# A row LSTM over images on one core: every 64-row product of the steady part made as two products of 64 output columns

## The chip, the cores and the metric

The kernel runs on one core of a Trainium2 chip. What is measured is the device time of one execution in microseconds. Engines are named as in the profile: PE is TensorE (PEld its weight loads), DVE is VectorE, ACT is ScalarE, POOL is GpSimd, SP is SyncE, which issues the DMA transfers.

## What is computed

The input x has 8 images of 96 channels, 128 rows and 128 pixels, in float32. It is normalised in 32 groups of channels per image. A masked convolution along each row makes four gates for every channel, and an LSTM runs down the rows: row r needs the hidden state h of row r - 1, through another convolution of three taps. The output is x plus all h.

```python
x = x + _L0_conv_ref(_gn(x), W_is, b_is, W_ss, b_ss)

its = conv(X, W_is * mask) + b_is            # 96 -> 384 channels, 1 x 3, causal in the pixels
def step(carry, row_in):                     # once for each of 128 rows
    h, c = carry
    ss = conv(h, W_ss) + b_ss                # 96 -> 384 channels, 3 taps
    gates = ss + row_in
    g5 = gates.reshape(B, 3, 4, Oc, Wd)      # Oc = 32: three thirds, four gates
    f, i, o = sigmoid(g5[:, :, 0]), sigmoid(g5[:, :, 1]), sigmoid(g5[:, :, 2])
    g = tanh(g5[:, :, 3])
    c_new = f * c + i * g
    h_new = o * tanh(c_new)
    return (h_new, c_new), h_new
```

The rows are a chain of 128 steps, and all arithmetic is float32.

## The kernel before

**Half-steps.** The eight images are two sets of four. A half-step is one row of one set: `HalfStep(n)` for n from -2 to 255, even n for the first set, odd n for the second (the first is one row ahead). While one set's elementwise work runs, the other set's products do. The code writes the order of the instructions of PE, ACT, DVE and POOL by hand: the string `PERIOD` (line 775) lists the pieces of a half-step with marks for which half-step they belong to, and `do` (line 803) issues them in that order. Lines 1175 and 1176 do so for n from 2 on; the last half-step has its own list.

**Products.** The 384 gate channels are three tiles A, B, C of 128, each with a PSUM bank of its own per half-step (`ps`, 128 partitions by 512 values: 256 for one half of the pixels, 256 for the other). The three-tap convolutions are rewritten over pairs of pixels, so that each tile takes seven kinds of products: "1", "2", "0" and "3" from the hidden state (moving operands `vs`, `vf` and the two parts of `vd`, made on DVE and POOL, lines 639 to 650), and "P", "Q" and "E" from the input (`xs`). All go through `HalfStep.mm` (lines 482 to 500, the matmul at 492): `rows` says which partitions of the weights and of the moving operand take part.

**Lanes.** In the steady part no product uses all 128 rows of the array. `piece` (line 508) makes each of "1", "2", "0", "3" as two products of 64 rows, one of partitions 0 to 63 and one of 64 to 127, and each of "P", "Q", "E", whose operand is 64 channels, as one product of 64 rows; `xs` holds these channels twice, so that either half of the rows will do. The class `Lanes` (line 407) chooses the half, mostly by the marks `<` and `>` in `PERIOD`, so that products of both halves alternate. Where two products in a row write the same bank from different halves, `mm` lets the later one wait until the earlier has ended (lines 489 to 491): `self.writer[a]` keeps the rows of the bank's last product and its number.

**After the products.** ACT adds the bias and copies one half of a bank (`copy`, line 563), DVE adds and subtracts (`even`, `odd`, lines 567 and 571), ACT makes tanh and sigmoid (lines 575, 587), DVE and POOL the cell (lines 592 to 611), ACT its tanh, DVE h (line 624), and DVE and POOL the moving operands of the next row. SP issues all transfers.

Of the kernel before, what the change touches and what calls it, by code (L numbers as in the profile page):

```python
# [21 lines left out]
def kernel(  # L22
# [29 lines left out]
    nc = tc.nc  # L52
    B, C, H, W = x.shape
    P = 128
    NH = 2
# [193 lines left out]
    class Scale:  # L249
# [23 lines left out]
        def mm(self, o, i, rhs, start=False, stop=False):  # L273
            nc.tensor.matmul(o, gm[:, i, :], rhs, start=start, stop=stop, skip_group_check=True)  # L274
# [110 lines left out]
    HB = BH * J  # L385
    NT = NB * R
    last = NT * NH - 1
# [54 lines left out]
    def hold(made, until):  # L442
        if until.ins.engine != E.Pool:
# [6 lines left out]
                reason="GpSimd starts when VectorE is done with both SBUF reads",  # L450
            )

    residuals = []
    lanes = Lanes()
    whole = slice(0, P)

    class HalfStep:
# [24 lines left out]
        def mm(self, a, half, weights, rhs, rows=slice(0, P)):  # L482
            self.take_bank(a)
            new = a not in self.started
            self.started.add(a)

            lo, hi = self.images.get(a, (0, BH))
            cols = slice(lo * J, hi * J)
            before = self.writer.get(a)
            if before is not None and before[0] != rows and whole not in (before[0], rows):  # L490
                lanes.wait(before[1])
            made = nc.tensor.matmul(  # L492
                self.ps[a][:, bass.ts(half, HB)][:, cols],
                weights[rows, bass.ts(a, P)],
                rhs[rows, cols],
                start=new,
                stop=False,
                skip_group_check=True,
            )
            self.writer[a] = rows, lanes.issued(made)  # L500

        def own(self, a, i):
# [579 lines left out]
    n = m = 0  # L1082
# [39 lines left out]
    rows = ring[2][:, 0 : (R - 1) * BH * (W + 1)].rearrange("p (r q) -> p r q", q=W + 1)  # L1122
# [109 lines left out]
```

## Time and profile before

| what | value |
|---|---|
| three runs | 1959.95, 1960.5, 1963.89 us; median 1960.5 us |
| the profiled execution | span 1964.8 us; no other time of it is given |
| PE, PEld busy | 1907.0 us (97%), 1821.3 us (93%), 17450 instructions each |
| DVE, ACT, POOL busy | 1799.9 us (92%), 1566.5 us (80%), 1354.5 us (69%) |
| granted TensorE clock, mean | 0.996 |
| line 492 in the chain that ended last | 93% |
| DMA | 234.64 MB, mean 119 GB/s |

The page shows the busy time of each engine, the same in 40 slices of the span, and the chain of work that ended last, followed back from the end: what stands in it set the time. A group of instructions is a line with what is written and read, the count, the busy time together, the mean length of one and the idle time before. In the groups of PE, "64*128" are the rows and columns of the array, and "64x256" partitions and columns of the moving operand. The timeline gives start and length of single instructions or of runs of equal ones. Matmuls are pipelined: the recorded length of one reaches into the next, and starts tell more than lengths.

### The profile page before, as it was taken

Reading aid. Unit: us, or ns where it says so; the run is one execution under the profiler, and the core shown is the slowest. Engines: PE = TensorE matmul, PEld = TensorE weight load, DVE = VectorE, ACT = ScalarE, POOL = GpSimd, SP = SyncE. Lnnn points to the kernel's source line nnn. Section 1 sums busy time; section 2 is a strip of 40 time slices with the busy share of each in tenths; the row PEclk is TensorE's granted clock in tenths of the full one; section 3 lists DMA queues with packets and bytes.
Section 4 is the critical chain, followed back from the end, with each engine's and each line's share of the span. In section 5 each row is a group of like instructions: output and inputs, shape, how many; then the busy total and the mean of one; then the engine's idle time right before and its main releaser. Section 6 shows DMA issues by size and latency. Waiting matters only on the chain.

```text
span 1964.8 us, 46182 instructions
## 1 busy us (share of the span) xinstructions
PE 1907.0 (97%) x17450; PEld 1821.3 (93%) x17450; DVE 1799.9 (92%) x4014; ACT 1566.5 (80%) x3501; POOL 1354.5 (69%) x1645
## 2 busy tenths in 40 slices
PE   3799999999999999999999999999999999999998
PEld 0469999999999999999999999999999999999997
DVE  5788999999999999999999999999999999999998
ACT  6678888888888887887888788888888878888886
POOL 3447777777777777777777777777777777777751
PEclk9989999999999999999999999999999999999999
DMA  9994424544443454444345443434544443354411
GB/s 401 412 300 101 113 73 113 119 98 101 100 110 89 100 119 98 109 92 115 86 97 119 98 116 88 116 89 90 119 104 112 92 108 96 84 119 111 106 33 33
DMA packets 101293, 234.64 MB, mean 119 GB/s; under 512 B 5840, under 2 KB 7376, under 8 KB 95056
## 3 DMA queue, kind: packets, MB, share of 16 engines
q1 hardware_dynamic: 101072, 231.70, 45.5%
q8 instruction: 138, 2.26, 0.5%
q14 instruction: 83, 0.68, 0.1%
HBM read 181.34 MB, written 50.33 MB: 118 GB/s over the span
## 4 chain that ended last, share of the span: by engine, by line
PE 94%; DMA 3%; ACT 1%; DVE 1%; issue 0%; POOL 0%; SPq 0%; DVEq 0%; POOLq 0%; ACTq 0%
PE ps L492 93%; DMA xs<-in_x_dram 3%; DVE bst L1113 1%; PE rows L198 0%; ACT xs L239 0%; ACT xs L240 0%; ACT g L575 0%; PE dm L183 0%; PE pv L274 0%; DVE hx L624 0%; ACT ps L587 0%; SPq L1100 0%; ACT piece L239 0%; POOL xw L320 0%; PE rows L183 0%
## 5 line engine op out<-in xcount | busy, mean ns | idle before, releaser
L492 PE MATMUL ps<-vd,wl 64*128 64x256 f32 (+1 forms) x6080 | 1190.5, 376 | 2.0 <-DVE ps L571 2.0
L492 PEld LDWEIGHTS ps<-vd,wl 64*128 64x128 f32 (+1 forms) x6080 | 870.8, 186 | 21.1 <-DVE ps L571 4.6
L492 PE MATMUL ps<-vs,wm 64*128 64x256 f32 (+1 forms) x3046 | 821.3, 377 | 2.9 <-POOL vs L639 2.2
L492 PE MATMUL ps<-vf,wm 64*128 64x256 f32 (+1 forms) x3046 | 767.0, 377 | 0.1
L492 PE MATMUL ps<-xs,wx 64*128 64x128 f32 (+1 forms) x3582 | 747.2, 348 | 1.8 <-POOL xs L337 1.8
L492 PEld LDWEIGHTS ps<-xs,wx 64*128 64x128 f32 x3582 | 605.6, 188 | 7.5 <-POOL xs L337 3.3
L587 ACT ACTIVATE ps<-ps 96x512 f32<-96x512 f32 (+1 forms) x768 | 388.4, 506 | 227.6 <-PE ps L492 219.0
L492 PEld LDWEIGHTS ps<-vs,wm 64*128 64x128 f32 (+1 forms) x3046 | 529.0, 186 | 13.9 <-POOL vs L639 3.4
L575 ACT ACTIVATE g<-ps 32x256 f32<-32x256 f32 (+1 forms) x1021 | 468.8, 482 | 19.3 <-PE ps L492 0.6
L492 PEld LDWEIGHTS ps<-vf,wm 64*128 64x128 f32 (+1 forms) x3046 | 460.3, 186 | 20.2 <-DVE vf L643 1.1
L492 PE MATMUL ps<-xs,wt 64*128 64x256 f32 x1518 | 449.3, 377 | 0.0
L563 ACT ACTIVATE m<-ps,wl 128x256 f32<-128x256 f32 x766 | 363.2, 474 | 102.8 <-PE ps L492 78.4
L647 POOL TENSOR_TENSOR vd<-hx 128x512 f32<-128x512 f32 x257 | 287.8, 1120 | 179.5 <-DVE vs L639 172.0
L567 DVE TENSOR_TENSOR ps<-m,ps 128x256 f32<-128x256 f32 x768 | 324.3, 423 | 82.4 <-ACT m L563 82.3
L571 DVE TENSOR_TENSOR ps<-m,ps 128x256 f32<-128x256 f32 x768 | 327.2, 426 | 17.7
L665 DVE TENSOR_TENSOR x<-x,hx 96x512 f32<-96x512 f32 x253 | 339.6, 1342 | 0.0
L320 POOL TENSOR_SCALAR xw<-xr,rstd,nmr 128x512 f32<-128x512 f32 (+1 forms) x264 | 207.5, 787 | 127.0 <-DVE x L665 113.9
L320 POOL TENSOR_SCALAR hx<-x,rstd,nmr 32x512 f32<-32x512 f32 (+1 forms) x244 | 218.9, 897 | 77.1 <-POOL xs L341 53.5
L341 POOL TENSOR_TENSOR xs<-xw 128x512 f32<-128x512 f32 (+1 forms) x254 | 271.2, 1068 | 0.0
L492 PEld LDWEIGHTS ps<-xs,wt 64*128 64x128 f32 x1518 | 264.8, 187 | 0.9 <-issue 0.3
L599 POOL TENSOR_TENSOR g<-i,g 96x256 f32<-96x256 f32 x251 | 182.5, 727 | 119.0 <-ACT g L575 110.6
L616 ACT ACTIVATE th<-c 96x256 f32<-96x256 f32 (+1 forms) x509 | 191.4, 419 | 2.7 <-DVE c L611 2.3
(101 smaller groups left out, 1506.0 us busy)
## 6 DMA issues: line engine op xcount, KB each, us to landing
xr<-in_x_dram SPq DMA_DIRECT2D x124, 512.0 KB, 6.9
x<-in_x_dram SPq DMA_DIRECT2D x62, 768.0 KB, 7.4
out_dram<-x SPq DMA_DIRECT2D x62, 768.0 KB, 4.7
xs<-in_x_dram SPq DMA_DIRECT2D x31, 1024.0 KB, 10.7
piece<-in_x_dram SPq DMA_DIRECT2D x16, 1024.0 KB, 10.8
x<-in_x_dram SPq DMA_DIRECT2D x62, 256.0 KB, 4.8
out_dram<-x SPq DMA_DIRECT2D x2, 576.0 KB, 3.7
xs<-in_x_dram SPq DMA_DIRECT2D x2, 512.0 KB, 8.2
```

Source lines behind the costliest of these rows:

```text
L320: return engine.tensor_scalar(dst, src, scale, shift, ALU.mult, ALU.add)
L341: engine.tensor_sub(differences, strided(xw[:, 0, :], 0, [(W + 1, n), (J, 2), (1, J)]), strided(xw[:, 0, :], J + 1, [(W + 1, n), (0, 2), ( ...
L492: made = nc.tensor.matmul(self.ps[a][:, bass.ts(half, HB)][:, cols], weights[rows, bass.ts(a, P)], rhs[rows, cols], start=new, stop=False, ...
L563: nc.scalar.activation(self.m1[a], m1, AF.Identity, bias=column)
L567: nc.vector.tensor_add(self.ps[a][:, 0:HB], self.m1[a], self.ps[a][:, HB:])
L571: nc.vector.tensor_sub(hi, self.m1[a], hi)
L575: nc.scalar.activation(self.part(g, lo, hi, t), self.part(ps, lo, hi, t), AF.Tanh)
L587: nc.scalar.activation(to, gate, AF.Sigmoid)
L599: nc.gpsimd.tensor_mul(to, i, g)
L616: nc.scalar.activation(self.part(self.th, lo, hi, t), self.part(self.c, lo, hi, t), AF.Tanh)
L647: diff = nc.gpsimd.tensor_sub(self.operand("vd", 2)[:, :, lo:hi], strided(h, 1, [(BH * JP - 1, 2), (JP, hi - lo), (1, J)]), strided(h, 0, ...
L665: residuals.append(nc.vector.tensor_add(xo, xo, self.h))
```

## The change

In half-steps 3 to 253 (`n_split`: `NH` is 2 and `last` is 255) each product of 64 rows is issued as two. The first takes the first 64 of the tile's 128 weight columns and writes partitions 0 to 63 of the bank, the second takes the other 64 columns and writes partitions 64 to 127. Both read the same 64 rows of the same moving operand, and both start or add to the bank's sums as the one did. The bank's last writer is now the second of the two. Products outside these half-steps, and products of 128 rows, are issued as before.

```diff
+    def n_split(n):
+        return NH < n < last - 1
+
...
             before = self.writer.get(a)
             if before is not None and before[0] != rows and whole not in (before[0], rows):
                 lanes.wait(before[1])
-            made = nc.tensor.matmul(
-                self.ps[a][:, bass.ts(half, HB)][:, cols],
-                weights[rows, bass.ts(a, P)],
-                rhs[rows, cols],
-                start=new,
-                stop=False,
-                skip_group_check=True,
-            )
+            parts = 2 if rows != whole and n_split(self.n) else 1
+            for q in range(parts):
+                wide = P // parts
+                made = nc.tensor.matmul(
+                    self.ps[a][bass.ts(q, wide), bass.ts(half, HB)][:, cols],
+                    weights[rows, bass.ds(a * P + q * wide, wide)],
+                    rhs[rows, cols],
+                    start=new,
+                    stop=False,
+                    skip_group_check=True,
+                )
             self.writer[a] = rows, lanes.issued(made)
```

On PE, the place where half-step 28 ends its products of `vs` and half-step 29 has begun those of `xs`: `ps2_0_15` is the bank of tile C of the first set in row 15, `ps1_1_14` and `ps2_1_14` are banks of the second set in row 14, and the shape is that of what is written. Before:

```order
L492 MATMUL ps2_0_15_3055<-vs_0_15_3110,wm_66 128x256
L492 MATMUL ps1_1_14_3108<-xs11_77,wx_67 128x256
L492 MATMUL ps2_1_14_3144<-xs11_77,wx_67 128x256 [waits PE_49,Activation_49]
L492 MATMUL ps2_0_15_3055<-vs_0_15_3110,wm_66 128x256 [waits PE_49]
L492 MATMUL ps2_1_14_3144<-xs11_77,wx_67 128x128
L492 MATMUL ps0_0_15_3084<-xs01_75,wt2_65 128x256 [waits DVE_49]
```

The same six products after the change:

```order
L498 MATMUL ps2_0_15_3890<-vs_0_15_3962,wm_66 64x256 x2
L498 MATMUL ps1_1_14_3959<-xs11_77,wx_67 64x256 x2
L498 MATMUL ps2_1_14_4013<-xs11_77,wx_67 64x256 [waits PE_49,Activation_49]
L498 MATMUL ps2_1_14_4013<-xs11_77,wx_67 64x256
L498 MATMUL ps2_0_15_3890<-vs_0_15_3962,wm_66 64x256 [waits PE_49]
L498 MATMUL ps2_0_15_3890<-vs_0_15_3962,wm_66 64x256
L498 MATMUL ps2_1_14_4013<-xs11_77,wx_67 64x128 x2
L498 MATMUL ps0_0_15_3928<-xs01_75,wt2_65 64x256 [waits DVE_49]
L498 MATMUL ps0_0_15_3928<-xs01_75,wt2_65 64x256
```

The order of the products stays; each stands there twice, the two halves one behind the other, and a wait stays on the first of them. The other engines keep their instructions and their order.

## The prediction

> **What bounds the kernel now.** I read the whole page first (engine totals, the slices, the chain that ended last), then the chain in order of time, then one half-step in the timeline. The page and the chain:
>
> ```profile
> span 1964.8 us, 46182 instructions
> PE 1907.0 (97%) x17450; PEld 1821.3 (93%) x17450; DVE 1799.9 (92%) x4014; ACT 1566.5 (80%) x3501; POOL 1354.5 (69%) x1645
> PE   3799999999999999999999999999999999999998
> PEclk9989999999999999999999999999999999999999
> ...
> 161.88 7.49 PE ps L492 x66
> 169.40 1772.87 PE ps L492 x16396
> 1942.31 5.46 PE ps L492 x34
> ```
>
> From 169.4 us to 1942.3 us the chain is nothing but matmuls of line 492: no wait for another engine stands in it for 1772.87 us, and the clock is at full speed. VectorE at 92% is a close second by share, but nothing in this stretch waits for it on the path. TensorE's "busy" alone would not tell that it is at its limit, so the next view is a stretch of the timeline, first the matmuls, then the weight loads:
>
> ```profile
> 827.29 0.38 PE L492 MATMUL ps<-vd,wl 64*128 64x256 f32 x1
> 827.39 0.38 PE L492 MATMUL ps<-vs,wm 64*128 64x256 f32 x1
> 827.50 0.38 PE L492 MATMUL ps<-vf,wm 64*128 64x256 f32 x1
> 827.61 0.38 PE L492 MATMUL ps<-vs,wm 64*128 64x256 f32 x1
> 827.72 0.38 PE L492 MATMUL ps<-vf,wm 64*128 64x256 f32 x1
> 827.82 0.38 PE L492 MATMUL ps<-vd,wl 64*128 64x256 f32 x1
> 827.93 0.38 PE L492 MATMUL ps<-vs,wm 64*128 64x256 f32 x1
> 828.04 0.38 PE L492 MATMUL ps<-vd,wl 64*128 64x256 f32 x1
> ```
>
> ```profile
> 827.39 0.19 PEld L492 LDWEIGHTS ps<-vs,wm 64*128 64x128 f32 x1
> 827.50 0.19 PEld L492 LDWEIGHTS ps<-vf,wm 64*128 64x128 f32 x1
> 827.72 0.18 PEld L492 LDWEIGHTS ps<-vd,wl 64*128 64x128 f32 x1
> 827.72 0.18 PEld L492 LDWEIGHTS ps<-vs,wm 64*128 64x128 f32 x1
> 827.83 0.19 PEld L492 LDWEIGHTS ps<-vd,wl 64*128 64x128 f32 x1
> ```
>
> One product of the program is two records here: the totals have 17450 matmuls and as many loads for half as many products. I call each record a pass. The passes of two products are woven into each other: vs at 827.39 and 827.61 is one product in one half of the rows of the array (a lane), vf at 827.50 and 827.72 another in the other lane. Within a lane the starts are 0.22, 0.21 and 0.22 us apart (827.39, .61, .82, 828.04; and 827.50, .72, .93), though each pass is recorded as 0.38 us long, so the recorded length overlaps its successor. The rate is what counts: 16396 passes in 1772.87 us over two lanes are 2 x 1772.87 / 16396 = 0.216 us per pass and lane. The lanes run without gaps; that is the bound.
>
> The loads tell the other half. Each starts with a matmul's start (827.50 beside 827.50) or a hair behind it, and runs under that matmul: it fills the lane for the next pass. Where its data come late (the two at 827.72, one of which would have been due at 827.61) the matmul behind it still starts at its place, 827.82. So a load is hidden as long as it is sent while the pass before it runs.
>
> What a load costs when nothing hides it is seen in one place, the start, where products of 64 columns are shorter than their loads:
>
> ```profile
> 144.06 0.52 PEld L492 LDWEIGHTS ps<-xs,wx 64*128 64x128 f32 x8 [0.33 <-issue]
> ...
> 144.50 0.19 PEld L492 LDWEIGHTS ps<-xs,wt 64*128 64x128 f32 x1
> 144.50 0.19 PEld L492 LDWEIGHTS ps<-xs,wx 64*128 64x128 f32 x1
> 144.61 0.19 PEld L492 LDWEIGHTS ps<-xs,wt 64*128 64x128 f32 x1
> 144.62 0.19 PEld L492 LDWEIGHTS ps<-xs,wx 64*128 64x128 f32 x1
> ```
>
> Eight loads, four in each lane, take from 144.06 to 144.50, and the next follow 0.11 us later: a load of 64 rows by 128 columns holds its lane 0.11 us, of which the recorded 0.19 is the longer, overlapping form.
>
> **The change part by part.** How many products are split comes from the groups that keep shapes apart:
>
> ```profile
> L492 PE MATMUL ps<-vd,wl 64*128 64x256 f32 x6016 | 1174.5, 376 | 0.0
> L492 PE MATMUL ps<-vs,wm 64*128 64x256 f32 x3012 | 809.6, 376 | 0.1
> L492 PE MATMUL ps<-vf,wm 64*128 64x256 f32 x3012 | 755.8, 377 | 0.1
> L492 PE MATMUL ps<-xs,wx 64*128 64x256 f32 x2562 | 594.7, 379 | 1.8 <-POOL xs L337 1.8
> L492 PE MATMUL ps<-xs,wt 64*128 64x256 f32 x1518 | 449.3, 377 | 0.0
> L492 PE MATMUL ps<-xs,wx 64*128 64x128 f32 x1004 | 191.3, 271 | 0.0
> ...
> L492 PE MATMUL ps<-xs,wh 64*128 64x256 f32 x36 | 7.7, 479 | 0.1
> ```
>
> The 256-wide groups sum to 16156 passes, 8078 products, and 50 of these lie outside the steady part and stay whole (the program's order has 50 unsplit ones); the 128-wide one is 502 products, all split. So 8530 products become 17060, and 17060 passes become 34120, each with a load of its own.
>
> 1. The work in the array. A pass of a half has the same 256 moving columns, so I keep 0.216 us for it. If the two halves, which use the same rows but different columns of the array, run at the same time, this term is zero; if they take turns in their lane, every product costs its lane 0.432 us more. No row shows two products in the same rows at once. I take zero, because two products in different rows do run at once above without lengthening each other, and price the other end as a rival.
>
> 2. The loads. The halves are written one behind the other: load, matmul, load, matmul of the left half, then the same of the right. If a lane takes its instructions in this order, the second pass of the left half must wait 0.216 us for the first, and only when it has started is the right half's first load sent. That load has nothing to hide under in its own columns: these are idle and wait for it. The same happens at each change from one half to the other. So each of the 17060 halves pays one exposed load. Bounds: 0 if the load is sent early; 0.19 if it costs what is recorded for one. I take half of the measured 0.11, 0.055 us, since half the columns are loaded and this row is the nearest (if the time of a load does not depend on its columns it is 0.11). A product then holds its lane 2 x (0.216 + 0.055) = 0.542 in place of 0.432, +0.110 us. For a 128-wide one: now load-bound at 2 x 0.11 = 0.22, then 2 x (0.11 + 0.055) = 0.33, +0.11 too. Sum: 8530 x 0.110 over two lanes = 469 us.
>
> 3. Instructions to fetch and send. Per pass TensorE must be handed a load and a matmul; today such a pair every 1772.87 / 16396 = 0.108 us suffices, afterwards a pair each 0.054 us would be needed to keep pace with the array, or 0.068 with term 2. The eight pairs at 144.06 went out in 0.44 us, 0.055 each, but they were few, and came after a wait of 0.33 us. So the price per pair lies between 0.055 and 0.108 us, and the time from nothing to the doubling of the steady part. I take nothing: the nearest row is the 0.055, below the 0.068 that term 2 leaves. It is the second largest doubt.
> The Trainium skill bears on this: "TensorE: Matmul & The Clock Gate", section "Wait — 56ns, not 53.3ns?", has about 62 ns of the sequencer per MATMUL where the hardware decoder is off, as the bound once a matmul is shorter than that. By that figure 34120 matmuls take 2115 us and the whole about 2285 (an estimate by that page) in place of term 2's sum; the trace cannot show which decoder is on, only that a load and a matmul together fit into 108 ns.
>
> 4. Waits and the other engines. The waits stay on the first of the two halves and their number is the same; what is behind a waiting load in the queue is now twice as many instructions but the same products. The second half ends a bank later than the product did, so ScalarE's and VectorE's readers start later by at most one pass per product chain. Those are off the path as long as TensorE is the slower, and slower it gets: VectorE's 1799.9 us of work gains slack. Nothing charged. The cover is TensorE's own slowness; without it VectorE would be next, at 92%.
>
> 5. The start before 160 us and the last half-steps keep their whole products: nothing.
>
> Sum, in the profiled execution: 1964.8 + 469 = 2434 us; the median of the runs, 1960.5, lies 4.3 below this execution, so I forecast **2430 us**. The half-step shows it directly:
>
> ```profile
> 1000.98 0.73 POOL L599 TENSOR_TENSOR g<-i,g 96x256 f32<-96x256 f32 x1 [0.23 <-ACT g L575]
> ...
> 1008.12 0.73 POOL L599 TENSOR_TENSOR g<-i,g 96x256 f32<-96x256 f32 x1 [0.44 <-ACT g L575]
> ```
>
> GpSimd's one product per half-step recurs after 7.14 us; with 251 half-steps, 469 us more make it 9.0.
>
> **The rivals.**
> - Not slower. All four quarters of the array run at once and each right-half load is sent while the left half still works. Place: the loads of the right half start with, or before, the left half's second matmul. Then a pass stays 0.216 and the time stays 1960; only the 1004 narrow passes lose their load bound (0.11 to about half of 0.216), at most 1 us. It decides if the array takes a load for idle columns past a matmul that still waits, as it now takes the loads of one lane past the other lane's waiting matmul (both loads at 827.72 are sent before either lane's next matmul). Against it: that jump is between rows, not within them. A real gain needs the pass itself to get below 0.216: I know of no row for that, and give 1% (20 us) as its size.
> The Trainium skill, "TensorEngine Tiling (Array Packing)", section "Tiling Modes", Key Properties, says of four 64x64 tiles that they are independent and may load and multiply in parallel; by that rule this rival holds and the sum is 1960 instead of 2430. The trace agrees for tiles in different rows and shows none in the same rows.
> - Taking turns. The two halves of a product share one stream of moving data per lane and run one after the other: 8028 x 0.432 + 502 x 0.22 us over two lanes, +1789, so 3750. For it: nothing in the trace has two streams in the same rows. Against: it would make the column position useless.
> - Bound by issue. At a price p per pair the steady part takes 34120 x p: with the 171 us around it (1960.5 - 1789) 0.07 gives 2560, 0.09 gives 3240, 0.105 gives 3750.
> - A smaller loss, 0.2% to 10% (up to 2160): loads partly hidden, or semaphores that fire later because the right half ends later.
>
> **How the numbers follow.** Exposed loads: 0.38, with 0.04 to 0.07 us per load 2300 to 2560. Bound by issue: 0.20. Taking turns: 0.13. A smaller loss: 0.08. All four at once with no change: 0.15; with a gain: 0.06. Under 0.2% a difference cannot be told from none here (the three runs spread by that). Faster 0.06, same 0.15, slower 0.79. Leaving out turns (0.13) and the gain (0.06), the range goes from the unchanged 1957 to the issue bound at about 0.095 us per pair, 3400. Of the slower cases alone, exposed loads have 2300 to 2560.
>
> **What would show it.** Right: 34120 matmul records of 64*64 on the product's line; in a lane four starts about 0.22, 0.05, 0.22, 0.05 apart in the order left, left, right, right; a right-half load that starts with the left half's second matmul; GpSimd's product every 9.0 us; readers on ScalarE waiting longer for TensorE. Term 1 wrong: no two passes of the same weights' two halves overlap. Term 2 wrong: right-half loads start beside the left half's, and the period is near 7.1. Term 3 wrong: idle columns with no load waiting, pairs evenly spaced, TensorE idle "by issue". Above all the forecast fails if the order in which a lane takes its instructions is not the program's.

## The result, and the profile after

The changed kernel takes 1974.24 us (median of 4 runs, 1972.7 to 1978.66) beside 1962.2 us for the kernel before on the same chip: a ratio of 1.0065, 95% interval 1.0043 to 1.0086. A second measurement (e9_again below) gives 1.0060, 1.0047 to 1.0073. The change is slower by about 12 us, not by the 469 that I forecast. The profiled execution has a span of 1970.9 us, only 6.1 more than the one of before; but that one had a slow start: GpSimd's fourth regular product stands at 187.78 us in it and at 181.05 us here.

The page of the changed kernel: engine totals, the clock, and the two DMA queues that matter (packets, MB, share of time):

```profile
span 1970.9 us, 80552 instructions
PE 1904.7 (97%) x34510; PEld 1686.7 (86%) x34510; DVE 1801.1 (91%) x4014; ACT 1565.9 (79%) x3501; POOL 1360.3 (69%) x1645
...
PEclk9999999999999999999999999999999999999999
...
q1 hardware_dynamic: 101072, 231.70, 45.2%
q8 instruction: 271, 4.44, 1.0%
...
L498 PEld LDWEIGHTS ps<-vd,wl 64*64 64x64 f32 (+1 forms) x12096 | 714.2, 133 | 81.2 <-issue 11.5
```

The passes did double: 34510 matmuls, that is 17450 + 17060. Yet TensorE is recorded as busy for 2 us less, so the doubled passes share the time of the old ones. A load of 64x64 is recorded with 133 ns where one of 64x128 had 186. And there is twice as much program to bring in: 271 packets of instructions with 4.44 MB, where the page of before has this row:

```profile
q8 instruction: 138, 2.26, 0.5%
```

4.44 MB in 271 packets are 16.4 KB each. The change adds 17060 loads and 17060 matmuls, and 133 packets: 34120 / 133 is 256.5, and a count at the gaps, below, makes it 256 instructions to a packet.

Now the place that the prediction looked at. The timeline of the changed kernel, first matmuls, then loads ("x2" are two records; their common length is that of one, so they start within the rounding of each other):

```profile
827.11 0.38 PE L498 MATMUL ps<-xs,wx 64*64 64x256 f32 x2
827.18 0.38 PE L498 MATMUL ps<-xs,wt 64*64 64x256 f32 x2
827.32 0.38 PE L498 MATMUL ps<-xs,wx 64*64 64x256 f32 x2
827.39 0.38 PE L498 MATMUL ps<-xs,wt 64*64 64x256 f32 x2
827.54 0.38 PE L498 MATMUL ps<-xs,wx 64*64 64x256 f32 x2
```

```profile
827.18 0.14 PEld L498 LDWEIGHTS ps<-xs,wt 64*64 64x64 f32 x2
827.33 0.14 PEld L498 LDWEIGHTS ps<-xs,wx 64*64 64x64 f32 x2
827.39 0.14 PEld L498 LDWEIGHTS ps<-vd,wl 64*64 64x64 f32 x2
```

I read each row of two as the left and the right half of one pass (e5_same_columns below, which puts the halves into the same columns, bears this out). `xs,wx` is one lane (827.11, .32, .54), `xs,wt` the other (827.18, .39): a pass still takes its lane 0.21 to 0.22 us, and in that time both halves are done. Their loads come in pairs too, each pair beside the matmuls that it hides under (827.18 beside 827.18, 827.33 beside 827.32). So in the regular part the change costs nothing. GpSimd's product, once per half-step, says the same:

```profile
1005.87 0.73 POOL L605 TENSOR_TENSOR g<-i,g 96x256 f32<-96x256 f32 x1 [0.38 <-ACT g L581]
...
1034.37 0.73 POOL L605 TENSOR_TENSOR g<-i,g 96x256 f32<-96x256 f32 x1 [0.38 <-ACT g L581]
```

Three rows between them are left out, so four half-steps take 28.50 us, 7.125 each. In the kernel before four of them, from 1000.98 on, end here:

```profile
1029.52 0.72 POOL L599 TENSOR_TENSOR g<-i,g 96x256 f32<-96x256 f32 x1 [0.42 <-ACT g L575]
```

That is 28.54, 7.135 each. The medians over all half-steps are 7.125 and 7.133: the regular half-step became 8 ns shorter, 2.0 us over 251. Where the 12 us are lost is seen in the chain in order of time:

```profile
162.73 19.43 PE ps L498 x352
182.16 1.32 issue
183.48 633.99 PE ps L498 x11695
817.55 113.64 PE ps L498 x2096
931.19 1.51 issue
932.70 113.64 PE ps L498 x2096
...
1562.17 1.39 issue
1563.56 173.69 PE ps L498 x3198
```

The one piece of 1772.87 us is broken into eleven, with "issue" between them: time in which TensorE waited for nothing that the profile shows. The view of the waits from 300 to 1900 us counts these places; in the kernel before it has no row of this kind:

```profile
PEld ps L498 <- issue: 11.5, 11, 2.0
PE ps L498 <- issue: 6.6, 7, 1.5
```

(us in total, times, longest.) The two rows overlap, since a matmul waits for its load. The whole loss shows in the half-steps: 244 of them, between the starts of GpSimd's fourth product and its fourth from the end, take 1752.99 us (181.05 to 1934.04) and took 1740.53 (187.78 to 1928.32), 12.5 us more. At 7.125 each they would take 1738.50, so the gaps cost 14.5 us, and the shorter half-step gives 2.0 back.

What TensorE lacks there is instructions. One gap, as the timeline has it:

```profile
930.60 0.59 PE L498 MATMUL ps<-vd,wl 64*64 64x256 f32 x3
932.70 0.43 PE L498 MATMUL ps<-vd,wl 64*64 64x256 f32 x1 [1.51 <-issue]
```

A product has four passes now, and this one is torn after the third. Its place is no accident. I counted TensorE's records of the trace (loads, matmuls, semaphore instructions) that start before each of the ten gaps of over 0.4 us between matmul starts in the steady part: the counts are 1985, 26305, 30657 and so on, and each is 193 plus a multiple of 256. So every gap stands at a seam between two packets of 256 instructions; the 12 such gaps of e9_again and the 13 of e12_no_stores below stand there too.

The ten microseconds ahead of this gap, as the view of the DMA queues has them:

```profile
DMA packets 1139, 2.19 MB, mean 219 GB/s; under 512 B 71, under 2 KB 71, under 8 KB 1139
...
q1 hardware_dynamic: 1139, 2.19, 101.6%
```

These are 919.6 to 929.6 us. There is no row of the instruction queue: not one packet of it started, while block transfers filled all 16 engines. SyncE had issued these around the start of that stretch, as its timeline shows (the store of an output block, the raw rows of the next input, the residual's rows):

```profile
916.35 0.33 SPq L674 DMA_DIRECT2D out_dram<-x  x1
917.28 2.33 SPq L160 DMA_DIRECT2D xr<-in_x_dram  x2
921.96 0.32 SPq L168 DMA_DIRECT2D x<-in_x_dram  x1
922.33 0.42 SPq L169 DMA_DIRECT2D x<-in_x_dram  x1
```

A half-step has 34 products (8530 / 251), now 68 halves of two passes, each pass a load and a matmul: 272 instructions, so a packet of 256 lasts 6.7 us. In this trace the packets from 200 to 1900 us are 6.7 us apart in the mean, but up to 12.0 apart at such a burst; in the kernel before the mean is 13.2 and the largest 19.5. All ten gaps follow a packet that started 9.8 to 12.0 us after the one ahead of it, and each ends 1.3 to 1.7 us after that packet's end.

A late packet alone makes no gap: of the 26 in this stretch that started more than 9.5 us after the one ahead, nine have one. What counts is the time left. From the twelfth packet on, a packet starts 0.7 us (median) after TensorE has reached the seam before it, and up to 5.9 us at a burst; it then moves for some 1.2 us, and TensorE goes on some 1.4 us after its end. The next seam is due 6.7 us after the one before: 5.9 + 1.2 + 1.4 is 8.5 us, 1.8 too many, and the longest gap is 1.9. In the kernel before a packet starts up to 5.3 us late at the same bursts, but it lasts twice as long, and the packet for the next seam is there at least 6.3 us ahead.

### The profile page after: what moved, and what is told of

It is laid out like the page before. It is cut to its first block, busy times and chain, and to the rows that moved or that the text cites. A ratio compares the mean times of both kernels' runs of the same rounds, so it can differ in the third digit from the quotient of the medians.

```text
span 1970.9 us, 80552 instructions
## 1 busy us (share of the span) xinstructions
PE 1904.7 (97%) x34510; PEld 1686.7 (86%) x34510; DVE 1801.1 (91%) x4014; ACT 1565.9 (79%) x3501; POOL 1360.3 (69%) x1645
## 3 DMA queue, kind: packets, MB, share of 16 engines
q8 instruction: 271, 4.44, 1.0%
## 4 chain that ended last, share of the span: by engine, by line
PE 93%; DMA 3%; ACT 2%; DVE 1%; issue 1%; POOL 0%; SPq 0%; POOLq 0%; DVEq 0%; ACTq 0%
PE ps L498 92%; DMA xs<-in_x_dram 3%; DVE bst L1119 1%; ACT xs L239 0%; ACT xs L240 0%; ACT g L581 0%; PE rows L198 0%; ACT ps L593 0%; ACT piece L239 0%; DVE hx L630 0%; PE pv L274 0%; POOL xw L320 0%; DVE c L617 0%; SPq L1106 0%; ACT xr L208 0%
## 5 line engine op out<-in xcount | busy, mean ns | idle before, releaser
L498 PE MATMUL ps<-vd,wl 64*64 64x256 f32 (+1 forms) x12096 | 1208.9, 376 | 8.0 <-issue 5.1
L498 PE MATMUL ps<-vs,wm 64*64 64x256 f32 (+1 forms) x6058 | 832.9, 376 | 3.0 <-issue 1.6
L498 PEld LDWEIGHTS ps<-vd,wl 64*64 64x64 f32 (+1 forms) x12096 | 714.2, 133 | 81.2 <-issue 11.5
L498 PE MATMUL ps<-vf,wm 64*64 64x256 f32 (+1 forms) x6058 | 777.1, 376 | 1.5 <-issue 1.2
L498 PE MATMUL ps<-xs,wx 64*64 64x256 f32 (+2 forms) x7096 | 759.0, 346 | 1.8 <-POOL xs L337 1.8
L498 PEld LDWEIGHTS ps<-xs,wx 64*64 64x64 f32 (+1 forms) x7096 | 483.6, 133 | 17.9 <-POOL xs L337 3.3
L498 PE MATMUL ps<-xs,wt 64*64 64x256 f32 (+1 forms) x3024 | 458.3, 376 | 0.1
L498 PEld LDWEIGHTS ps<-vs,wm 64*64 64x64 f32 (+1 forms) x6058 | 409.3, 132 | 42.0 <-POOL vs L645 2.5
L498 PEld LDWEIGHTS ps<-vf,wm 64*64 64x64 f32 (+1 forms) x6058 | 355.8, 132 | 60.9 <-DVE vf L649 1.8
L498 PEld LDWEIGHTS ps<-xs,wt 64*64 64x64 f32 (+1 forms) x3024 | 210.6, 133 | 2.5 <-issue 0.9
```

Source lines behind the costliest of these rows:

```text
L498: made = nc.tensor.matmul(self.ps[a][bass.ts(q, wide), bass.ts(half, HB)][:, cols], weights[rows, bass.ds(a * P + q * wide, wide)], rhs[ro ...
```

## The experiments

The theory after these traces, "late instructions": in the array the halves cost nothing, and the loss is packets of instructions that come late during bursts of block transfers. Its rival: a cost of the split products themselves, spread over all half-steps. All diffs are against the changed kernel unless said otherwise, and "..." stands for lines left out.

**The same again.** No edit.

> The changed kernel once more, on the chip of the other two, for the number of its gaps and its time: about 1974 us, 8 to 12 gaps over 0.4 us after 170 us, at half-steps 7 and 0 mod 8.

Measured: 1973.7 us (1965.5 to 1974.89), 1.0060 (1.0047 to 1.0073). The waits on "issue" from 300 to 1900 us are again 12.1 us in 12 pieces, but most are at other times than in the first trace. A fixed place in the program would not move.

**Fewer transfers, halves.** The output is stored for the last block only, and the raw rows of the input are loaded for one row of four.

```diff
     def load_rows(s, k, lo=0, hi=R):
+        hi = 1 if k > 1 else hi
...
     def store(s, k, lo, hi, first=0, end=BH):
+        if k + 1 < NB:
+            return
```

> The changed kernel with all steady half-steps split, but the block stores are left out except the last block's, and the loads of the rows for the input products bring one row of four: of a burst of 2.8 MB some 1.3 MB are left. The output is therefore not written for the most part, and input rows repeat. 'Late instructions': no gap over 0.4 us after 170 us or at most two, the regular half-step stays 7.125, and the time is 2 us below the kernel before (about 1960). 'Waits': nothing on the engines changes, so the time stays near 1974.

Measured: 1958.61 us, ratio 0.999 (0.998 to 1.0). The whole loss is gone, and the chain has its one piece back:

```profile
162.60 1770.73 PE ps L499 x32793
```

32793 passes without a break, 2 x 2 x 1770.73 / 32793 = 0.216 us per pass and quarter of the array. In the window from 919.6 to 929.6 us, where the changed kernel got no packet of instructions, this one got two:

```profile
q1 hardware_dynamic: 28, 0.04, 1.4%
q8 instruction: 2, 0.03, 1.3%
```

**Fewer transfers, whole products.** The same two edits in the kernel before. If less traffic helped any kernel, the run above would prove nothing.

> The kernel before (whole products) with the transfers thinned as in the thinned run of the changed kernel: the output block is stored for the last block only, and the normalised input's raw rows are loaded for one row of four; the output is therefore not the reference's. Theory 'late instructions' (the loss of the change lies wholly in packets of instructions that the bursts of transfers delay, and the split itself saves 8 ns a half-step): the whole products have no gaps to lose, so the half-step stays at 7.133 us and the time within 0.1% of 1960.5 (1958.5 to 1962.5), that is 1 to 3 us above the thinned changed kernel's 1958.6. Rival 'the transfers cost every kernel' (memory traffic slows the other engines or the products, and thinning helps both kernels alike): about 12 us less, 1949 to 1951.

Measured: ratio 1.0005 (0.9996 to 1.0013), median 1962.67 us. Without split products the transfers cost nothing, so the 15 us between e9_again and e3_less_dma are what the bursts cost the split ones (14.5 by the half-steps above). Against each other the two thinned kernels have ratios of 0.999 and 1.0005; that the split alone gains a little agrees with their half-steps (7.125 and 7.13 us), but the intervals overlap, and I don't claim it.

**Stores left out alone.** The second of the two edits, in the changed kernel.

> The changed kernel without the stores of all blocks but the last; the loads are whole, so the output is not the reference's but the next rows' input is. Theory 'the burst counts as a whole' (the packet is late because some 2.8 MB are under way at once): the store is about a third of the burst, the gaps shrink but some stay, 1962 to 1970, with gaps of 0.2 to 1 us. Rival 'the stores delay the packet': the gaps go as in the thinned run, 1958 to 1960. Rival 'the loads alone do it': the gaps stay at ten or so of 0.4 to 1.9 us, 1971 to 1975.

Measured: 1976.2 us, ratio 1.0079 (1.0066 to 1.0092), a little above the range of "the loads alone do it" and far from the other two: leaving the stores out wins nothing. The gaps have moved to the bursts as they now are:

```profile
PEld ps L498 <- issue: 13.4, 13, 1.8
```

One burst of loads is under way from 983 us on. From 981 to 992 us, ahead of a gap of 1.5 us that begins at 993.4, the DMA queues have again one row, and it is not that of the instructions:

```profile
q1 hardware_dynamic: 946, 1.84, 73.6%
```

Stores without loads were not tried, so whether a burst of stores could do the same is open. So is what the packet waits for in a burst, the DMA engines, the memory or a place in a queue: no record parts these.

**Both halves on the same columns.** The two halves of a product are put into the same 64 columns of the array (one lane into the left, the other into the right). The sums of a bank are then not the reference's; loads and matmuls are as many and as long as in the changed kernel.

```diff
+            side = self.Side(rows) if split else None
...
-                    self.ps[a][bass.ts(q, wide), bass.ts(half, HB)][:, cols],
+                    self.ps[a][bass.ts(side if split else q, wide), bass.ts(half, HB)][:, cols],
```

> Both halves of a split product go to the same 64 columns of the array: those of the lower rows to output partitions 0 to 63, those of the upper rows to 64 to 127. As many instructions, loads and passes as in the changed kernel, but the sums are not the reference's. If it is the column position that lets the halves run side by side, they now take turns in their lane: 4 x 0.216 us for a product, a half-step of about 14.2 us, 3740 us in all, which is the price that the prediction put on taking turns. If passes of one lane overlapped for another reason, the half-step stays near 7.1.

Measured: 3747.12 us, one run (as in the other two kernels of which no ratio is given). GpSimd's product recurs after twice the time:

```profile
1011.61 0.72 POOL L611 TENSOR_TENSOR g<-i,g 96x256 f32<-96x256 f32 x1 [6.35 <-ACT g L587]
1025.86 0.73 POOL L611 TENSOR_TENSOR g<-i,g 96x256 f32<-96x256 f32 x1 [6.33 <-ACT g L587]
```

14.25 us is 2 x 7.125. This is my rival "taking turns", 3750, made to happen; it shows that the different columns are what lets the halves run together. It shows more: here the halves do take turns, and still not one load is exposed, since the half-step is twice the regular one to the hundredth. By step 2's 0.055 us for each of the 34 halves that a lane has in a half-step it would be 1.9 us longer.

**Four quarters.** Each product as four of 32 columns.

```diff
-            parts = 2 if rows != whole and n_split(self.n) else 1
+            parts = 4 if rows != whole and n_split(self.n) else 1
```

> Every product that the change makes as two is made as four of 32 output columns: four times the instructions of before, a packet of 256 every 3.3 us if TensorE keeps pace. Theory A (all column tiles run side by side, and only instructions that come late cost time): between bursts the half-step stays at 7.12 us, in each of the some 60 bursts TensorE loses about 3 to 6 us more than now, 2150 to 2350 us in all. Theory B (sending a load and a matmul has a price of its own between 0.027 and 0.054 us, which the change just escaped): the half-step is longer everywhere, 272 pairs times the price: at 0.04 us 10.9 us and 2900 in all, at 0.054 14.7 us and 3860.

Measured: 2551.13 us, at a granted clock of 0.954. The waits from 300 to 1900 us and the DMA queue:

```profile
PEld ps L498 <- issue: 340.8, 342, 5.9
PE ps L498 <- issue: 227.6, 111, 5.4
```

```profile
q8 instruction: 538, 8.81, 1.5%
```

The shortest half-steps take 7.123 us, no more than with two halves: 272 pairs of a load and a matmul are sent in that time, 0.026 us a pair. The median one takes 8.3. With 544 instructions a half-step a packet is needed every 3.35 us; the median spacing is 3.94. After 170 us 198 gaps of over 0.4 us, the longest 5.8, make 414 us together, of the some 590 that this run is longer, and 197 of them stand at a seam between packets. So the doubt of step 3 is real, but its limit is how fast instructions arrive and not how fast they are sent. Neither expected number is met (2150 to 2350, or 2900 and more). The mechanism is that of late instructions, now over the whole run; what the lower clock adds to it I have not parted from it.

**Half of the half-steps.** Two kernels, each with the split in four of every eight half-steps: those away from the bursts, and those around them.

```diff
-        return NH < n < last - 1
+        return NH < n < last - 1 and n % 8 in (1, 2, 3, 4)
```

> Half of the steady half-steps are split: those with n mod 8 in 1 to 4, away from the burst of block transfers that recurs every 57 us. Theory 'late instructions' (in the changed kernel TensorE runs dry where a 16 KB instruction packet comes 10 to 12 us after the one before it instead of 6.5, which is behind the burst of a block store and four block loads): here the gaps over 0.4 us in the matmul starts go from ten after 170 us to none or one, the regular half-step is 7.125 us where split and 7.133 where not, the time is that of before to within 0.1% (about 1961 against 1962). Rival 'waits' (splitting lengthens the chains that end a bank, wherever it is done): half of the loss stays, about +6 us, and gaps with it.

The other one has `n % 8 in (5, 6, 7, 0)`.

> The other half of the steady half-steps is split, n mod 8 in 5, 6, 7 and 0, those that run during or just before the burst. As many products are split as in the run away from the burst. 'Late instructions': nearly all gaps stay, at half-steps 7 and 0 mod 8, 0.5 to 1.9 us each, +9 to +12 us (about 1972). 'Waits': half of the loss, +6 us, the same as in the run away from the burst.

Measured: 2420.4 us (ratio 1.2339, 1.2322 to 1.2356) and 2427.07 us (1.2372, 1.2345 to 1.2398). Both theories missed by 450 us, in kernels that split half as much. What the two have in common is that whole and split products follow each other closely: the last pieces of one half-step stand among the first of the next, and the tile shape of TensorE's products changes 1340 times, where it does so 19 times in the fully split kernel. Both are hit alike by this, and it hides what they were made to show. One sign is left: e2_burst has four gaps of over 0.4 us in its steady part, 3.2 us together, all at seams between packets, and e1_calm has none at a seam. That fits late instructions; it is not the whole of the 7 us between the two.

**Narrow products alone.** To price such a change of shape: only the products of 128 moving columns, two in each half-step, are split. They stand in two places, so there are four changes per half-step, 1004 in all.

```diff
-            parts = 2 if rows != whole and n_split(self.n) else 1
+            parts = 2 if rows != whole and n_split(self.n) and hi - lo < BH else 1
```

> Only the 502 products with 128 moving columns are split, every product of 256 stays whole. If the 8 ns by which the regular half-step of the changed kernel is shorter (7.125 against 7.133) come from these, whose passes were bound by their loads, the half-step is 7.125 to 7.127 here, there are no gaps since instructions grow by 6% only, and the time is 2 us below before (1960 against 1962), which five rounds may or may not tell apart. If they come from the wide products, the half-step stays 7.133 and the time that of before.

Measured: 2291.21 us, ratio 1.1678 (1.1662 to 1.1694), with 1004 matmuls more than the kernel before. One such place in the timeline:

```profile
1002.53 0.59 PE L498 MATMUL ps<-vs,wm 64*128 64x256 f32 x2
1003.05 0.43 PE L498 MATMUL ps<-xs,wx 64*64 64x128 f32 x4
1003.42 0.48 PE L498 MATMUL ps<-vs,wm 64*128 64x256 f32 x1
1003.42 0.48 PE L498 MATMUL ps<-vd,wl 64*128 64x256 f32 x1
1003.74 0.38 PE L498 MATMUL ps<-vs,wm 64*128 64x256 f32 x1
```

While the four narrow passes run, from 1003.05 to 1003.42, no pass of the other lane starts, and the first whole pass after a change has its lane for 0.32 us (1003.42 to 1003.74) in place of 0.21. The half-step:

```profile
1006.76 0.73 POOL L605 TENSOR_TENSOR g<-i,g 96x256 f32<-96x256 f32 x1 [1.26 <-ACT g L581]
1015.22 0.73 POOL L605 TENSOR_TENSOR g<-i,g 96x256 f32<-96x256 f32 x1 [1.10 <-ACT g L581]
```

8.46 us, 1.33 more than 7.13, or 0.33 us per change of shape. That explains the two runs above: 1320 further changes by 0.33 are 436 us, and their half-steps from 200 to 2380 us are together 437 and 442 us longer than at 7.133 each (the whole runs are 460 and 466 us longer). From which products the 8 ns of the changed kernel come, which this run was made for, stays open.
The Trainium skill, "TensorEngine Tiling (Array Packing)", section "Tiling Modes", Key Properties, says that to change the tiling mode the engine must drain; these runs agree and give it a price.

**Split along the moving columns.** Each product as two with all 128 weight columns and half of the moving columns, so that the number of instructions is that of the change and the tile shape that of before.

```diff
+            wide = (cols.stop - cols.start) // parts
...
-                wide = P // parts
-                    self.ps[a][bass.ts(q, wide), bass.ts(half, HB)][:, cols],
-                    weights[rows, bass.ds(a * P + q * wide, wide)],
-                    rhs[rows, cols],
-                    start=new,
+                part = slice(cols.start + q * wide, cols.start + (q + 1) * wide)
+                    self.ps[a][:, bass.ts(half, HB)][:, part],
+                    weights[rows, bass.ts(a, P)],
+                    rhs[rows, part],
+                    start=new and q == 0,
```

> Each 64-row product of the steady part is split along its moving columns: two of 128 (or 64) moving columns, each with all 128 output columns. The number of instructions is that of the changed kernel, but both halves use the same part of the array, one behind the other, and each pass has a load of 128 columns (0.11 us) against 0.107 us of columns. A pass bound by its load at 0.112 gives a half-step of 68 x 0.112 = 7.6 us and about 2080 us; instructions are then fetched every 7.1 us and gaps as in the changed kernel may add 5 to 10 us. If loads of 128 columns were hidden by more than one pass, the half-step would be 68 x 0.109 = 7.4 us, 2030 us.

Measured: 2132.86 us, above both expected times.

```profile
1013.13 0.72 POOL L603 TENSOR_TENSOR g<-i,g 96x256 f32<-96x256 f32 x1 [0.82 <-ACT g L579]
1020.93 0.73 POOL L603 TENSOR_TENSOR g<-i,g 96x256 f32<-96x256 f32 x1 [0.97 <-ACT g L579]
```

7.80 us a half-step, 0.115 us for a pass of 128 columns: that agrees with a pass bound by its load of 64x128, which the start of the kernel had shown to hold the lane for 0.11. With the half-step longer, a packet lasts longer, and only three gaps are left, of 0.6 to 0.84 us. So the number of instructions alone does not cost the 12 us; it is this number in a half-step of 7.1 us.

**Moving half of the loads.** In the changed kernel, the raw rows of the second set are loaded a half-step later, to break up the burst; the edit also makes them wait for VectorE's newest residual addition.

```diff
+            if s == 1 and k > 2 and newest:
+                hold(made, newest[-1])
...
+        if r == 0 and s == 0 and k + 1 < NB:
+            rest = [(load_rows, 1, k + 1)]
```

> The changed kernel, all steady half-steps split, with the burst of block transfers pulled apart: the two loads of the second set's input rows (1 MB) are issued a half-step later, behind the block loads, and wait for a residual addition on VectorE. Bytes and all other work stay. 'Late instructions': the gaps over 0.4 us after 170 us fall from ten to three or fewer, the regular half-step stays 7.125 us, and the time is 1958 to 1963 us, below the changed kernel by 11 us or more. If it is the bytes over the whole 57 us and not the burst that delays the instructions, the gaps and the 1974 us stay.

Measured: 2028.06 us, ratio 1.0345 (1.0332 to 1.0358): a miss. The loads now come too late: GpSimd waits for them, and TensorE waits for VectorE, which it hardly did before:

```profile
POOL xw L322 <- DMA xr<-in_x_dram: 48.1, 14, 4.2
...
PEld ps L500 <- DVE vf L651: 31.1, 30, 1.3
...
PEld ps L500 <- DVE c L619: 18.7, 22, 1.7
...
PEld ps L500 <- issue: 9.4, 33, 1.5
```

**The same move in the kernel before.** This parts the two effects. The edits are those of e8_spread, with whole products.

> The kernel before (no product split) with the same two loads a half-step later: control for the run in which they are moved in the changed kernel. It has no gaps to lose, so its time is that of before to 0.1% and its half-step 7.133 us; if moving the loads saves time by itself, it shows here.

Measured: 2006.63 us, ratio 1.0232 (1.0219 to 1.0246). This too is a miss: the move costs 46 us by itself, with whole products. The run before it lies 21 us above that. It still has 9.4 us of waits on "issue", but only six of its gaps stand at a seam between packets, 5.7 us together in place of ten with 11.9; the others, and the rest of the 21 us, I have not explained. So the move did less than expected against late packets and cost more than they do. It is no remedy, and whether a gentler one exists (the same loads in smaller pieces, with no new wait) was not tried. At best it would bring the changed kernel 2 us, 0.1%, below the kernel before.

## Why the prediction was right or wrong

The sign was right; of the size nearly all was wrong, and at the place that I had named in the text as the forecast's main risk.

- Step 1, the work in the array: right. The halves run side by side and a pass stays at 0.216 us. Its other end, "taking turns", is what the array does when the columns are the same (3747 us).
- Step 2, the loads: this is the step that failed, and the whole forecast hung on it. I took 0.055 us for an exposed load of each half, on the ground that a lane takes its instructions in the program's order, and came to 469 us. Measured is 0: the right half's load and first pass run beside the left half's, 0.2 us ahead of the left half's second pass. No record shows in which order the program holds the four passes of a product, so it stays open whether the array takes them out of the order that I assumed or that order was wrong. I had seen such a jump between rows of the array (both loads at 827.72) and denied it between columns, with no row for that. "Term 2 wrong" in my list of signs described the trace after as it is.
- Step 3, instructions to fetch and send: taken as nothing, and measured as the whole loss, 14.5 us. I had looked only at the rate of sending. That rate is no limit: a pair every 0.052 us is kept up through each regular half-step (7.125 / 136), and 0.026 in e4_quarters. What I did not look at was the row of the instruction queue, which doubles, and what else is on the DMA engines when its packet is due. My sign for it, TensorE idle "by issue", is what the trace shows, but in ten places and not evenly.
The estimate of 2285 us by the Trainium skill's 62 ns per MATMUL ("TensorE: Matmul & The Clock Gate", section "Wait — 56ns, not 53.3ns?") does not hold here, as 11695 matmuls in 633.99 us are 0.054 us each.
- Step 4, waits and the other engines: right. ScalarE's wait for TensorE (line 587, now 593) went from 199.7 to 196.6 us between 300 and 1900 us, and that of line 563, now 569, from 57.2 to 64.0; neither is on the path.
- Step 5, start and last half-steps: right within what can be seen. GpSimd's first regular product stands at 159.71 us in the changed kernel and at 159.90 in e11_whole_less_dma, with whole products; in the profile of the kernel before it stands at 166.38, after a stretch (110 to 200 us) at a granted clock of 0.96 in place of 1.00. From the fourth product from the end to the end of the span it is 36.8 us, and 36.5 before.
- The rivals. "Not slower", which I gave 0.15, described the mechanism: all four quarters at once, and a gain of about 1 us (2 us measured, at 8 ns a half-step; that it comes from the narrow passes, as I wrote, is not shown). The time itself fell to "a smaller loss" (0.08), but by neither of the two causes that I gave it there. A gain of 2 us and a loss of 14.5 make the result. The right sign is luck: I forecast a loss from loads, and it came from instructions.

## What to carry to other kernels

In this kernel the two halves of a product ran at once in different columns, loads and all, although the kernel issues them one behind the other; so splitting a product by columns neither cost nor gave time to speak of where rows and columns were already full. Keep neighbouring products in one tile shape (each change between 64x128 and 64x64 cost 0.33 us here), and when a change doubles the instructions of the engine that bounds the kernel, look at the instruction queue: how long a packet lasts, and whether a burst of transfers can hold the next one up for nearly as long. To tell such gaps from others, count instructions: theirs lie a whole number of packets apart.

## What was not expected of the hardware

- A change of tile shape between products: 0.33 us (e7_narrow, and by the same price e1_calm and e2_burst).
- Instructions come as DMA packets of 256, each about when TensorE reaches the one before. In bursts of some 2 MB of block transfers a packet came up to 12 us after the last one, and TensorE ran dry by up to 1.9 us, always at the seam of two packets; with whole products the same bursts cost nothing that was measured (1.0005).
- The first passes of both halves of a product start together, though the kernel issues the halves one behind the other, and a load is hidden under a matmul of its own rows.
The Trainium skill, "TensorE: Matmul & The Clock Gate", section "The mechanism", has matmuls start and end strictly in the order of the program; whether these starts break that rule depends on the order of the passes in the program, which no record shows. The list of that section also has loads overlap with matmuls only where the rows of the array differ, while its text lets a load for a background weight buffer go ahead too; in e5_same_columns loads stay hidden within one tile, which fits the second and not the first.
